# Attention and FFN in one kernel: when the products with the values are made, which PSUM banks the products share, and which engine standardises the layernorms

## Chip, core and metric

One core of a Trainium2 chip runs the whole program. The time is the device time of one execution in microseconds (us). It is told as the median of several runs; a profiled execution, of which the trace is, has a time of its own.

The engines by the names that the profile uses: PE is TensorE (matmuls; its weight loads are PEld), DVE is VectorE, ACT is ScalarE, POOL is GpSimd. SP issues all DMA transfers, in its program order.

## Reference

Sixteen sequences of 256 tokens with 256 channels go through one transformer layer, in float32:

```python
x = x + attn(layernorm(x))            # 16 heads of 128, 4 key/value heads
x = x + ffn(layernorm(x))             # one linear 256 -> 256, 8-bit integers
# attn: q, k, v = x wq^T, x wk^T, x wv^T;  scores = q k^T / sqrt(128)
#       a query sees the last 32 keys (itself among them) and the first 4 ("sinks")
#       softmax over these, times v, all heads times wo^T
# ffn:  weight rows and x rows scaled to -128..127 and rounded; integer product; scaled back; + bias
# layernorm: (x - mean) / sqrt(var + 1e-5), no weights
```

## The kernel before

**Units and visits.** A unit is one sequence n and one key/value head g with its four query heads: 64 units, numbered i = 4n + g. The main loop makes one visit for each unit but the last two (i = 0 to 61). The last two units of sequence 15 are cut by halves of the tokens instead of by heads, and stand with the rest of the end behind the loop. The kernel's order is the written order: `in_written_order` ties every engine's instructions to the order in which the program makes them. So each engine works through its own list, and waits where an operand or a buffer isn't ready.

**A visit** i, in TensorE's order:

1. `unit_scores(i)`: the scores `pss` of unit i. Queries are taken in blocks of 16 tokens, four heads at a time (64 columns of weights), against 52 keys (48 of the window, 4 sinks): 32 matmuls of 128x64 weights (L592). DVE scales and masks them into SBUF (L598) and takes the maxima (L607); ACT makes eight exponentials with their sums (L612).
2. `queries(i + 1, 0)`: two heads of the next unit's queries, `pq`. For sequences 1 to 15 a product of 2x2 blocks is made of seven block products instead of eight (`products`, `combine`, Winograd's form): seven products in two PSUM banks, 28 matmuls, since `mm` cuts each into two of 64 columns (L90). ACT copies the first product (L336), DVE makes five additions out of the banks into `qt` (L321 to L325). One such pass of five is "a half of the queries".
3. the first part of the output projection `py` of unit i - 3 (`projected_fast`, parts 0 and 1, again by seven products; 24 and 32 matmuls).
4. `times_values(i - 2)`: the products with the values, `po`: 64 matmuls with 52 rows and 64 columns of weights (L684), into two banks. ACT copies the two banks to `oT` (L695), and POOL makes four sums `os` of it (L286 to L289), which the output's second part multiplies.
5. the other half of the queries, `queries(i + 1, 1)`, then the output's second part.
6. a "chunk": in turn the keys or the values of two heads of the next sequence (`pk`, `pv`; 28 matmuls). ACT copies both banks in the next visit (`both_banks`, L342), POOL adds them up (L321 to L325), and for keys ACT spreads them into the windows `kt` (L447, L448). Values go through DRAM (`vd`) to `vw`, the layout that `po` needs.
7. every fourth visit, the FFN's product `pa`.

**Softmax's way.** `normalised` (L620 to L626) scales the exponentials by their sums on DVE and transposes them in blocks of 32 (`z`). SP stores `z` to DRAM (`zd`) and loads it back in another order (`ad`, four transfers) in the next visit (`ways`). `po` reads `ad` and `vw`.

**Layernorms.** `statistics` makes means and variances on DVE and 1/sqrt on POOL (L213 to L218); `standardise` makes (x - mean) times 1/sqrt on DVE in one operation per tile of 128 tokens (L223). That is done once for the attention (`norm`) and once for the FFN (`ffn_steps`). Both results are transposed by way of DRAM (`turned_by_blocks`: z_xnT and z_hb out, xnT and hb back). In between, the FFN's `quantise` takes DVE and POOL (L803, L806, L807), `narrow` casts `hb` on ACT (L828), `rest` scales `pa` on DVE (L848).

**Where such steps stand.** `at(place, point, f)` puts a step into visit `place` at a named point; `do` runs it there. For the FFN a `plan` lists step, visit after the sequence's output, and point.

**PSUM.** Eight banks: one for scores (`ps_s`), one for transposes and `pa` (`ps_t`), two for the output (`ps_y`), two for the queries (`ps_q`, tags q0 and q1) and two in rotation for `po`, keys and values (`ps_m`). A pool gives a buffer anew only when its last reader is done.

Of the kernel before, what the change touches and what calls it, by code (L numbers as in the profile page):

```python
# [34 lines left out]
def kernel(  # L35
# [14 lines left out]
    P = 128  # L50
# [33 lines left out]
    ps_q = ctx.enter_context(tc.tile_pool(name="ps_q", bufs=1, space=bass.MemoryType.PSUM))  # L84
    ps_m = ctx.enter_context(tc.tile_pool(name="ps_m", bufs=2, space=bass.MemoryType.PSUM))
# [122 lines left out]
    def statistics(src, tiles, tag, eng=pool):  # L208

        st = p2.tile([P, NT, nc.vector.BN_STATS_DIM], FP, tag="st", name=f"st_{tag}")  # L210
        mv = p3.tile([P, NT, nc.vector.BN_AGGR_DIM], FP, tag="mv", name=f"mv_{tag}")
        for j in tiles:
            dve.bn_stats(st[:, j, :], src[:, j, :])  # L213
        for j in tiles:
            dve.bn_aggr(mv[:, j, :], st[:, j, :])
        js = slice(tiles[0], tiles[-1] + 1)
        eng.tensor_scalar(mv[:, js, 1], mv[:, js, 1], LN_EPS, None, ALU.add)
        pool.tensor_tensor(mv[:, js, 1], mv[:, js, 1], half[:, js], ALU.pow)  # L218
        return mv
# [4 lines left out]


# [49 lines left out]

    def q_banks(name):
        return [ps_q.tile([P, 4, P], FP, tag=f"q{k}", name=f"{name}_{k}") for k in range(2)]
# [94 lines left out]
    def norm_stats(n):  # L372
        mvs[n] = statistics(xts[n], range(NT), f"a{n}")

    def norm(n, t):
        if t == 0:
            xns[n] = p1.tile([P, NT, DM], FP, tag="xn", name=f"xn_{n}")
        standardise(xns[n], xts[n], mvs[n], [t])
# [158 lines left out]
    def queries(n, g, half_of, plain=False):  # L537
# [6 lines left out]
        if n > 0 and not plain:  # L544
            p = q_banks(f"pq_{n}_{h}")
# [5 lines left out]
        if plain:  # L551
            pq = ps_m.tile([P, 4, P], FP, tag="m", name=f"pq_{n}_{h}")
        else:
            pq = ps_q.tile([P, 4, P], FP, tag=f"q{half_of}", name=f"pq_{n}_{h}")
# [23 lines left out]
    def unit_scores(i):  # L578
# [4 lines left out]
        if i == U - 1:  # L583
            pss = ps_q.tile([P, 4, P], FP, tag="q0", name=name).rearrange("p a b -> p (a b)")[:, 0 : NK2 * NK]
# [56 lines left out]
    def turned_twice(i, sm):  # L641
# [21 lines left out]
        def turn(a):  # L663
            pz = turned[a] = ps_q.tile([P, 4, P], FP, tag=f"q{a}", name=f"pz_{i}_{a}")
# [64 lines left out]
    def projected(n, g, t):  # L729
# [12 lines left out]
        if g == G - 1 and not last:  # L742
            return lambda: dve.tensor_add(xts[n][:, t, :], xts[n][:, t, :], py)

    def projected_fast(i, part):
# [16 lines left out]
        if (g, part) == (G - 1, 1):  # L762
# [3 lines left out]
            def rest():  # L766
                sums.first()
                sums.combine(dve)
# [3 lines left out]
            return rest  # L772
# [5 lines left out]
    def ffn_steps(n):  # L778
# [9 lines left out]
        def stats():  # L788
            got.append(statistics(xt, tiles, f"f{tag}"))

        def norm():
            standardise(h, xt, got[0], tiles)
# [67 lines left out]
    def last_steps(j):  # L860
# [36 lines left out]
        def turn():  # L897
            for c in range(NC):
                pt = ps_q.tile([P, 4, P], FP, tag=f"q{c}", name=f"ht_{tag}_{c}")[:, 0]
# [39 lines left out]
    VALUES, OUTPUT = 2, 3  # L939

# [9 lines left out]
    at(0, "early", lambda: norm(1, 0))  # L950
    at(0, "early", lambda: norm(1, 1))
    at(1, "turn", lambda: turned(1))
    for n in range(2, B):
        p = (n - 1) * G
        if n > 2:
            at(p - 4, "load", lambda n=n: load_x(n))
        at(p - 3 + (n == 2), "gap", lambda n=n: norm_stats(n))
        at(p - 2, "gap", lambda n=n: norm(n, 0))
        at(p - 2, "early", lambda n=n: norm(n, 1))
# [15 lines left out]
    for n in range(B - 1):  # L975
        p = n * G + G - 1 + OUTPUT
# [7 lines left out]
        if by_dma(n):  # L984
            plan = (("stats", 1, "gap"), ("norm", 1, "late"), ("scale", 2, "early"), ("quantise", 2, "early"),
                    ("turn", 3, "turn"), ("out", 3, "early"), ("back", 3, "leave"), ("narrow", 4, "late"),
# [4 lines left out]
        if n == B - 3:  # L991
            ffn_last_but_one = step
            plan = plan[:7]
# [29 lines left out]

    for i in range(U - NT):
        do(i, "load")
        if i - 1 in ways:
# [16 lines left out]
        first = queries(*units[i + 1], 0)  # L1043
# [5 lines left out]
        exps(range(1))  # L1049
        first.first() if isinstance(first, Products) else first()  # L1050
        exps(range(1, NK2))
        if isinstance(first, Products):
            first.combine(dve)
        rests, o = [], i - OUTPUT
        if o >= 0:
            if fast_output(units[o][0]):
                projected_fast(o, 0)
            else:
                rests.append(projected(*units[o], 0))
        do(i, "early")  # L1060
        values_out = times_values(i - VALUES) if i >= VALUES else None
        ways[i] = normalised(i, sm)
        if values_out:
            for f in values_out:
                f()
        second = queries(*units[i + 1], 1)
        second.first() if isinstance(second, Products) else second()
        if o >= 0:
            if fast_output(units[o][0]):
                rests.append(projected_fast(o, 1))  # L1070
            else:
                rests.append(projected(*units[o], 1))
        if isinstance(second, Products):
            second.combine(dve)
        for f in rests:
            if f:
                f()
# [10 lines left out]
        do(i, "leave")  # L1088
    assert not tasks and not waiting, sorted(tasks)
# [9 lines left out]
    exps_a(range(NK2))  # L1099
    for k in range(2):  # L1100
        normal_a(k)
    projected_fast(a - 3, 0)
    values_out = times_values(a - 2)
    values_out[0]()
    rest = projected_fast(a - 3, 1)
    rest()
    exps_b(range(NK2 // 2))
    values_out = times_values(a - 1)
    values_out[0]()
# [76 lines left out]
```

## Time and profile before

| what | value |
|---|---|
| median of 3 runs (lowest to highest) | 670.62 us (670.53 to 671.6) |
| the profiled execution's own time | 672.28 us |
| its span in the trace | 670.1 us |
| mean granted TensorE clock | 0.996 |
| DMA, mean over the span | 146 GB/s |
| mean of one po matmul (L684), of one pq matmul (128x128) | 221 ns, 273 ns |
| four visits, 300.1 to 339.4 us: DVE, ACT, POOL busy | 33.61, 23.55, 32.33 us |

How to read it: the page gives the busy time of each engine as a share of the span. TensorE's matmuls are pipelined, so 658.5 us "busy" doesn't say that each took its least time; the distance between the starts of neighbours does. The chain is followed back from the last instruction, at each step to what released it or to the instruction before it on its engine. In the timeline, neighbouring instructions of one kind are put together: start, length, engine, line, operation, tiles, how many, and in brackets an idle time of the engine before it with its releaser. "issue" as releaser means that the engine waited for nothing that the profile shows. Rows of groups give the busy time, the mean of one in ns, and the idle time before them.

### The profile page before, as it was taken

The numbers are of one execution on the slowest core, as the hardware profiler recorded it, in microseconds if no ns is written. First come the engines' busy times: TensorE is split into PE (matmuls) and PEld (weight loads), VectorE is DVE, ScalarE is ACT, GpSimd is POOL, SyncE is SP. The second block draws the span as 40 slices with busy tenths as digits, with TensorE's granted clock in tenths as the row PEclk, the third lists the DMA queues.
The fourth block names the chain that finished last, engine by engine and source line by source line (L and its number), as shares of the span: only waits on it lengthen the run. The fifth ranks groups of instructions, "written<-read, shape, count | busy, mean of one in ns | idle before, by whom it ended". The sixth has DMA issues, their size and how long they took to land.

```text
span 670.1 us, 35751 instructions
## 1 busy us (share of the span) xinstructions
PE 658.5 (98%) x14956; PEld 618.0 (92%) x14956; DVE 542.7 (81%) x1418; ACT 390.8 (58%) x1514; POOL 523.7 (78%) x795
## 2 busy tenths in 40 slices
PE   8999999999999999999999999999999999999995
PEld 6688899999999999999999999999999999999863
DVE  3766787888888898888889888888888889878665
ACT  3776465567566566655656656556756656656441
POOL 4788788787887978789787887978788797878534
PEclk9999999999999999999999999999999999999998
DMA  8558565656666566765666666566766656565520
GB/s 288 131 145 178 144 165 116 157 142 160 148 150 159 138 154 139 163 155 140 152 151 131 157 149 165 134 146 137 172 151 150 150 142 156 128 145 129 131 49 32
DMA packets 152928, 97.62 MB, mean 146 GB/s; under 512 B 69440, under 2 KB 143040, under 8 KB 152768
## 3 DMA queue, kind: packets, MB, share of 16 engines
q1 hardware_dynamic: 152768, 95.34, 59.8%
q8 instruction: 118, 1.93, 1.3%
q14 instruction: 42, 0.34, 0.2%
HBM read 59.11 MB, written 36.18 MB: 142 GB/s over the span
## 4 chain that ended last, share of the span: by engine, by line
PE 97%; issue 1%; DVE 1%; ACT 1%; POOL 0%; DMA 0%; POOLq 0%
PE pq L90 31%; PE py L90 30%; PE po L684 10%; PE pss L592 9%; PE pv L90 7%; PE pk L90 7%; PE pa L90 1%; PE pz L666 0%; ACT scores L612 0%; DMA x<-in_x_dram 0%; POOL mv_a L218 0%; ACT qt L563 0%; PE ht_last L900 0%; DVE xn L223 0%; PE pm L187 0%
## 5 line engine op out<-in xcount | busy, mean ns | idle before, releaser
L612 ACT ACTIVATE scores<-scores,nmax 128x52 f32<-128x52 f32 x512 | 166.7, 329 | 110.8 <-DVE nmax L607 108.7
L90 PE MATMUL pq<-xs,wq_sums 128*64 128x128 f32 x1416 | 118.0, 273 | 0.0
L612 ACT ACTIVATION_READ_ACCUMULATOR scores<-scores,nmax 128x1 f32 x512 | 97.1, 190 | 0.0
L90 PE MATMUL pq<-xnT,wq_sb 128*64 128x128 f32 (+1 forms) x1104 | 94.4, 295 | 0.0
L90 PE MATMUL py<-wo_sb,oT 128*64 128x128 f32 (+1 forms) x1152 | 88.9, 297 | 0.0
L90 PEld LDWEIGHTS pq<-xs,wq_sums 128*64 128x64 f32 x1416 | 86.3, 137 | 0.0
L90 PE MATMUL py<-wo_sums,os 128*64 128x128 f32 x1344 | 83.1, 273 | 0.0
L342 ACT COPY b_k<-pk 128x512 f32<-128x512 f32 (+1 forms) x60 | 31.9, 533 | 85.6 <-PE pk L90 83.6
L684 PEld LDWEIGHTS po<-ad,vw 52*64 52x64 f32 x4096 | 65.5, 134 | 12.5 <-issue 11.9
L90 PEld LDWEIGHTS py<-wo_sb,oT 128*64 128x64 f32 x1152 | 69.3, 137 | 7.5 <-issue 0.3
L90 PEld LDWEIGHTS py<-wo_sums,os 128*64 128x64 f32 x1344 | 75.4, 137 | 0.1
L684 PE MATMUL po<-ad,vw 52*64 52x64 f32 x4096 | 74.3, 221 | 0.0
L592 PE MATMUL pss<-kt,qt 128*64 128x52 f32 x2048 | 72.1, 223 | 0.6 <-issue 0.4
L592 PEld LDWEIGHTS pss<-kt,qt 128*64 128x64 f32 x2048 | 68.6, 138 | 3.6 <-ACT qt L563 1.6
L90 PEld LDWEIGHTS pq<-xnT,wq_sb 128*64 128x64 f32 x1104 | 61.6, 137 | 9.6 <-issue 0.7
L598 DVE SCALAR_TENSOR_TENSOR scores<-pss,masks 128x416 f32<-128x416 f32 x62 | 36.2, 583 | 40.7 <-PE pss L592 40.7
L695 ACT COPY oT<-po 128x512 f32<-128x512 f32 x124 | 65.4, 577 | 0.8 <-PE po L684 0.8
L323 DVE TENSOR_TENSOR qt<-pq,qt 128x256 f32<-128x256 f32 x118 | 50.2, 425 | 12.7 <-DVE qt L322 0.5
L321 DVE TENSOR_TENSOR qt<-pq,p_q 128x256 f32<-128x256 f32 x118 | 46.9, 397 | 14.4 <-ACT p_q L336 14.1
L286 POOL TENSOR_TENSOR os<-oT 128x256 f32<-128x256 f32 x56 | 42.8, 764 | 11.2 <-ACT oT L695 11.2
L623 DVE TENSOR_TENSOR scores<-scores,sm 128x416 f32<-128x416 f32 x62 | 49.3, 795 | 2.1
L447 ACT COPY kt<-k_line 128x1536 f32<-128x1536 f32 x32 | 47.3, 1477 | 0.4 <-POOL k_line L325 0.3
(186 smaller groups left out, 1564.1 us busy)
## 6 DMA issues: line engine op xcount, KB each, us to landing
vw<-vd SPq DMA_DIRECT2D x60, 336.0 KB
zd<-z SPq DMA_DIRECT2D x62, 256.0 KB
ad<-zd SPq DMA_DIRECT2D x248, 64.0 KB
vd<-vt SPq DMA_DIRECT2D x30, 256.0 KB
x<-in_x_dram SPq DMA_DIRECT2D x15, 256.0 KB
out_dram<-y SPq DMA_DIRECT2D x15, 256.0 KB
zd_xnT<-z_xnT SPq DMA_DIRECT2D x56, 64.0 KB
xnT<-zd_xnT SPq DMA_DIRECT2D x56, 64.0 KB
```

The costliest lines, as they stand in the source:

```text
L90: pe.matmul(to[c : c + HALF], left[:, c : c + HALF], right, start=start, stop=stop)
L286: pool.tensor_add(s[0], a21, a22)
L321: eng.tensor_add(c11_u, like(p[0][:, 0:2], c11_u), two(p1, c11_u))
L323: eng.tensor_add(c21_c22, like(p[1][:, 0:2], c21_c22), v.unsqueeze(1).to_broadcast(c21_c22.shape))
L342: act.copy(copies[k], self.p[k][:, 0 : 4 - k])
L447: act.copy(k[:, :, :, 0:NW], windows())
L592: pe.matmul(pss[j * HALF : (j + 1) * HALF, k, :], qt[n, g][:, t, bt].rearrange("p h i -> p (h i)"), kt[n, g // 2][:, g % 2, b, :], start=T ...
L598: dve.scalar_tensor_tensor(s[:, :, 0:NK], pss, SCALE, masks, ALU.mult, ALU.add)
L612: act.activation(s[:, k, 0:NK], s[:, k, 0:NK], AF.Exp, bias=nmax[:, k : k + 1], scale=1.0, accum_out=sm[:, k : k + 1],)
L623: dve.tensor_mul(s[:, :, 0:NK], s[:, :, 0:NK], sm.unsqueeze(2).to_broadcast([P, NK2, NK]))
L684: pe.matmul(po[j][d0 : d0 + HALF, k].rearrange("p (a y) -> p a y", a=2), vw[n, g // 2][r, kb, v0 : v0 + HALF], ad[k][r], start=True, stop= ...
L695: act.copy(to[:, j], po[j].rearrange("p k (h i) -> p k h i", i=QB))
```

## The change

- **Products with values.** Odd visits from 3 on make `po` of two units (i - 3 and i - 2) right after each other; even visits make none. Behind the loop, units 60 and 61 are made together as well. The output is one unit later: an even visit makes both parts of unit i - 4 and part 0 of unit i - 3, an odd one part 1 of unit i - 4.
- **Queries.** Both halves of the next unit's queries come at the start of the visit, ahead of the output; DVE adds them up one after the other.
- **PSUM.** `ps_q` is gone; `ps_m` has four banks in rotation for queries, `po`, keys, values and the transposes of the end.
- **Layernorm.** From the third sequence on, and in every FFN that goes through DRAM, ScalarE standardises: per tile one operation that adds the negated mean and one that multiplies. POOL negates the mean.
- **Places.** Statistics and norm move by a visit or to another point, and x is loaded a visit earlier; the FFN's steps are put elsewhere, and some of those of sequences 12 and 13 go behind the loop. The `ad` of a unit whose number is even is loaded at the end of the odd visit that follows it.

```diff
-    ps_q = ctx.enter_context(tc.tile_pool(name="ps_q", bufs=1, space=bass.MemoryType.PSUM))
-    ps_m = ctx.enter_context(tc.tile_pool(name="ps_m", bufs=2, space=bass.MemoryType.PSUM))
+    ps_m = ctx.enter_context(tc.tile_pool(name="ps_m", bufs=4, space=bass.MemoryType.PSUM))
...
+        if negated:
+            pool.tensor_scalar(mv[:, js, 0], mv[:, js, 0], -1.0, None, ALU.mult)
...
+    def standardise_act(dst, src, mv, tiles):
+
+        for j in tiles:
+            act.activation(dst[:, j, :], src[:, j, :], AF.Identity, bias=mv[:, j, 0:1], scale=1.0)
+        for j in tiles:
+            act.mul(dst[:, j, :], dst[:, j, :], mv[:, j, 1:2])
...
-            p = q_banks(f"pq_{n}_{h}")
+            p = m_banks(f"pq_{n}_{h}")
...
-        at(p - 3 + (n == 2), "gap", lambda n=n: norm_stats(n))
-        at(p - 2, "gap", lambda n=n: norm(n, 0))
-        at(p - 2, "early", lambda n=n: norm(n, 1))
+        at(max(p - 4, 1), "early", lambda n=n: norm_stats(n))
+        at(p - 2, "early", lambda n=n: norm(n))
...
-        p = n * G + G - 1 + OUTPUT
+        p = n * G + G + 3
...
-            plan = (("stats", 1, "gap"), ("norm", 1, "late"), ("scale", 2, "early"), ("quantise", 2, "early"),
-                    ("turn", 3, "turn"), ("out", 3, "early"), ("back", 3, "leave"), ("narrow", 4, "late"),
+            plan = (("stats", 1, "early"), ("norm", 2, "early"), ("scale", 2, "late"), ("quantise", 2, "late"),
+                    ("turn", 3, "early"), ("out", 3, "early"), ("back", 3, "leave"), ("narrow", 4, "late"),
                     ("linear", 5, "linear"), ("rest", 7, "early"), ("leave", 7, "leave"))
...
+    def output_parts(i):
+
+        if i % 2:
+            return [(i - 4, 1)]
+        return [(i - 4, 0), (i - 4, 1), (i - 3, 0)]
...
     for i in range(U - NT):
+        visit = i % 2 == 1 and i >= 3
         do(i, "load")
-        if i - 1 in ways:
+        if i - 1 in ways and not visit:
             ways.pop(i - 1)()
...
+        ps.append(queries(*units[i + 1], 1))
+        done = 0
+        for k, q in enumerate(ps):
+            exps(range(done, 1 + 3 * k))
+            done = 1 + 3 * k
+            q.first() if isinstance(q, Products) else q()
+        exps(range(done, NK2))
+        for q in ps:
+            if isinstance(q, Products):
+                q.combine(dve)
         do(i, "early")
-        values_out = times_values(i - VALUES) if i >= VALUES else None
+        rests = [r for r in (output_part(*o) for o in output_parts(i) if o[0] >= 0) if r]
+        for r in rests:
+            r[0]()
+        values_out = [times_values(u) for u in (i - 3, i - 2)] if visit else []
+        for r in rests:
+            r[1]()
         ways[i] = normalised(i, sm)
-        if values_out:
-            for f in values_out:
+        for k, v in enumerate(values_out):
+            for f in v:
                 f()
-        second = queries(*units[i + 1], 1)
...
         do(i, "leave")
+        if i - 1 in ways:
+            ways.pop(i - 1)()
...
     exps_a(range(NK2))
+    ffn_last_but_one("turn")
+    ffn_last_but_one("out")
+    ffn_last_but_one("back")
+    ffn_last_but_two("rest")
+    ffn_last_but_two("leave")
     for k in range(2):
         normal_a(k)
-    projected_fast(a - 3, 0)
-    values_out = times_values(a - 2)
-    values_out[0]()
-    rest = projected_fast(a - 3, 1)
-    rest()
+    for part in range(2):
+        output_part(a - 4, part)
+    output_part(a - 3, 0)
+    values_out = [times_values(u) for u in (a - 2, a - 1)]
+    for v in values_out:
+        v[0]()
+    for f in output_part(a - 3, 1):
+        f()
     exps_b(range(NK2 // 2))
-    values_out = times_values(a - 1)
-    values_out[0]()
```

## Prediction

> **What bounds the kernel now.** I read the page first: the share of each engine, and the chain that ended last.
>
> ```profile
> PE 658.5 (98%) x14956; PEld 618.0 (92%) x14956; DVE 542.7 (81%) x1418; ACT 390.8 (58%) x1514; POOL 523.7 (78%) x795
> ...
> PE 97%; issue 1%; DVE 1%; ACT 1%; POOL 0%; DMA 0%; POOLq 0%
> ```
>
> TensorE is the whole chain. So an edit pays only if it shortens TensorE's stream, and costs only if it makes TensorE wait. The wait table of the weight loads shows one wait that repeats:
>
> ```profile
> PEld po L684 <- issue: 11.9, 62, 0.4
> ```
>
> Sixty-two times, once a visit, the products with values (po) begin 0.19 us late for no releaser that the trace shows. The PE timeline of one visit says what surrounds them:
>
> ```profile
> 303.55 0.61 PE L90 MATMUL py<-wo_sums,oT 128*64 128x128 f32 x8
> 304.08 1.16 PE L684 MATMUL po<-ad,vw 52*64 52x64 f32 x64
> 305.17 0.66 PE L90 MATMUL pq<-xnT,wq_sb 128*64 128x128 f32 x8
> 305.66 0.61 PE L90 MATMUL pq<-xs,wq_sums 128*64 128x128 f32 x8
> 306.10 0.39 PE L90 MATMUL pq<-xs,wq_sb 128*64 128x128 f32 x4
> ```
>
> Eight matmuls of the 128x64 shape take 0.44 us where nothing changes (305.66 to 306.10), but 0.53 ahead of po and 0.49 behind it: the 52x64 shape costs at both ends. The start stamps of single matmuls give it exactly. Pairs of 128x64 matmuls follow each other at 102 ns (last start to first), groups of four po at 38. Into po it is 203 (101 too many), between po's first two groups 87 (49 too many), out of po 148 (110 over 38), between the first two pairs behind it 153 (51 too many). Together **0.31 us for each stretch of po**. A po stretch is alone its shape: 64 of them.
>
> A second thing: every fourth visit the score matmuls (pss) wait inside their stretch, 975 ns long instead of 869, because DVE's last sums of the queries end too late:
>
> ```profile
> 339.93 1.26 PE L592 MATMUL pss<-kt,qt 128*64 128x52 f32 x32
> ...
> 340.16 0.29 DVE L325 TENSOR_TENSOR qt<-pq,qt 128x128 f32<-128x128 f32 x1
> ```
>
> The sums of `qt` still run at 340.45 while the scores that read `qt` started at 339.93. That is 0.106 us in most of 14 places.
>
> **The change, part by part.**
>
> *Two units' po together.* The loop's 60 units come in 30 pairs (odd visits 3 to 61), and units 60 and 61 make one more behind the loop: 31 stretches fewer. 31 x 0.31 = **-9.6 us**. All of it lies on TensorE's path. If the second unit's 64 kept their own slow first group (49 ns) and were joined at 102 instead of 38 (64 ns more), 0.197 would be left, -6.1; I take 0.31, because within a stretch all later groups stand 38 apart.
>
> *Both halves of the queries early.* DVE sums both halves right after each other, some 3 us before the next scores. The 14 waits of 0.106 go: **-1.5** (bounds 0 and -1.8, with one longer wait at 70 us).
>
> *What the new order asks of the banks.* Per odd visit PE now writes ten banks from a rotation of four: q first (A,B), q second (C,D), po (A,B), po (C,D), chunk (A,B). I lay a clock from the visit's first pss matmul, with strides from the timeline: pss 0.92, 28 matmuls 1.54 or 1.53, 32 py 1.75 plus 0.10 entry, po 0.94 + 0.04. First po at 5.84, second at 6.82, chunk at 7.87, end 9.44. An even visit (80 py) takes 9.88, with pa 10.32. Four visits: 39.08, against 39.82 now (for instance 300.11 to 339.93): the same 0.74.
>
> DVE's side of the clock, from the rows of the visit that starts at 310.03:
>
> ```profile
> 310.03 1.09 PE L592 MATMUL pss<-kt,qt 128*64 128x52 f32 x32
> ...
> 311.17 0.59 DVE L598 SCALAR_TENSOR_TENSOR scores<-pss,masks 128x416 f32<-128x416 f32 x1 [0.94 <-PE pss L592]
> ...
> 312.47 0.34 ACT L612 ACTIVATE scores<-scores,nmax 128x52 f32<-128x52 f32 x1 [1.75 <-DVE nmax L607]
> ...
> 313.09 0.42 DVE L321 TENSOR_TENSOR qt<-pq,p_q 128x256 f32<-128x256 f32 x1 [0.18 <-ACT p_q L336]
> ```
>
> The first sums begin at 3.06; five of them take 1.77 and the next follow at 1.72, so the second half is done at 6.6. The first po (5.84) finds A,B free at 4.85; the second (6.82) finds C,D free 0.2 us ahead. That holds where DVE and ACT enter the visit on time. In the visit with g = 3 they don't: DVE carries y, two transposes and the normalisation of the visit before to its end, ACT two key and two value copies (1.57 + 0.96), so both start some 0.3 late, and the sums end at 6.9. I charge 0.2 in 14 visits, **+2.8** (bounds 0 and 0.4 each: 0 to 5.6).
>
> *Layernorm on ScalarE.* Two sequences' worth (attention and FFN) leave DVE per four visits: 2 x 2 x 0.62 to 0.80 (L223), off the path. ACT takes eight operations of 128x256 with a per-partition operand instead. No row shows one. Nearest rows:
>
> ```profile
> L612 ACT ACTIVATE scores<-scores,nmax 128x52 f32<-128x52 f32 x512 | 166.7, 329 | 110.8 <-DVE nmax L607 108.7 <-DVE st_f L213 2.0
> ...
> L704 ACT COPY oT<-po 128x256 f32<-128x256 f32 x8 | 2.4, 386 | 2.2 <-PE po L684 2.2
> ```
>
> L612 has such an operand; with 204 more columns at 0.84 ns (577 ns at 512 against 255 at 128) one is 0.50 long. Four L704 copies follow at 0.30. Four operations lie between 1.2 and 2.3 us; since L612 hides the read behind it (stride 0.325) I take 0.43 each, 1.7. The FFN's four stand in an odd visit (g = 1), between the exponentials (end at 5.36) and the copies of po, which can begin at 5.84 + 1.16 = 7.0: ACT is free at 7.1. The chunk wants bank A at 7.87, and gets it at 7.65. So nothing; the first block's second half of TensorE work (po of the second unit) hides it by 0.2, and each 0.1 us beyond costs 14 x 0.1 = 1.4. POOL gains one negation of two columns (0.22, L217's size) per layernorm, 0.44 in 39 us.
>
> [...]
>
> *Transfers.* SP's queue keeps its order within a visit; the two `ad` loads of a pair now wait at the end of an odd visit and the start of the next for buffers that the pair of po frees (8 us into the odd visit), and are read two visits later. Behind them stand vw (read three visits later) and zd_hb. The tightest is hb: zd_hb issued from 8.6 of visit g = 2, landed 4.5 us later, read back in 2.6 behind the `out` store, landed at some 8 of visit g = 3, where ACT casts it at 9.2. So nothing, by 1 us; if it is gone, ACT holds up the chunk's copies behind it, and the next queries.
>
> *The ends.* In the first visits the output and po of sequence 0 come one visit later, so visits 1 to 3 are shorter on TensorE while POOL makes weight sums (3.2 us each); what is lost there is in the bounds below. Output products of one more unit (56 matmuls, 3.05 us) move behind the loop, so the loop is shorter by as much; there they fill the 1.3 us in which PE waits for its transposes at 638.7. Against it, the FFN of sequence 13 now turns behind the loop: zd_hb, hb and the cast come through SP's queue behind four ad and six vw transfers. POOL's h is done some 5 us into the tail, SP reaches zd_hb at 6, writes 2.8, 2.7 to land (606.9 to 609.6 for zd), reads back 2.6 plus 2: 15.5 to 16.5 with the cast, where PE wants it at 15.3. **+0.7** (-1.5 to +3).
>
> Sum: -9.6 - 1.5 + 2.8 + 0.7 = **-7.6**. The profiled execution took 672.28 (span 670.1 and 2.2 around it), so 664.7; the median of three is 670.62, so **663.0**.
>
> **Rivals.**
>
> *Slower: POOL's queue reaches ScalarE's, and TensorE waits once in four visits.* Now POOL makes one unit's sums os a visit; afterwards two in a row, 5.8 us, and the key chunk's sums stand behind them. Place: sequence's second half. From the start of visit g = 1: ACT's layernorm 5.36 + 1.7 = 7.1; two po copies 8.1; eight os 13.9 (2.9 a unit, L286 to L289); h clipped and shifted 16.4 (2.4, L806, L807); key sums 19.4 (3.04, L321 to L325); key copies on ACT 21.0 (1.57, L447, L448); value-chunk copy 21.6; and its bank is what the second half of the queries wants in visit g = 3 at 9.44 + 9.88 + 2.46 = 21.8. The margin is 0.15. For it: POOL is 78% busy, and the layernorm row is missing from the trace. Against: each link is a measured stride but one. If the four operations take 2.4 and each POOL group its worst row (3.11 twice, 3.12), it is 1.2 late, 1.05 past the margin, 14 x 1.05 = +14.7: 677.7. It decides from 0.54 late past the margin (7.6/14).
>
> *Smaller gain: the switch isn't removed but moved.* The second po stretch waits for its banks at 0.4, and its first group is slow again (0.197 x 31 = 6.1): -6.1 - 1.5 + 5.6 + 0.7 = -1.3, 669.3. For it: four banks for ten uses. Against: DVE loses 2.4 to 3.2 us of layernorm per four visits.
>
> *Nothing (the change doesn't do what it says):* the 0.31 is a cost of po's own 64, not of the turn of shapes; then -1.5 + 0.7 and 0 to 2.8 are left, 669.8 to 672.6. Against: the start stamps show 203 into the 128x128 transposes (pa to pz) and 202 out of them too.
>
> **Numbers.** Forecast 659 to 667: 0.64. Small gain, 667 to 669.3: 0.16. Within 0.2% (what a measurement of this kernel can tell): 0.06. Slower: 0.14. Range 659 to 671: it leaves most of the slower case out, and reaches the forecast's lower bound (-9.6 - 1.8 - 0.2).
>
> **What would show it.** The wait of po for "issue" some 33 times instead of 62; po stretches of 128 with one 203 ahead; four visits in 39.1 to 39.4 us; no wait in pss. Wrong, if PE waits at pq for ACT b_v (g = 3), at po for DVE qt, or at pa in the tail for hT.

## The result, and the profile after

| what | before | after |
|---|---|---|
| median, same chip (lowest to highest) | 671.42 us (670.53 to 672.6) | 728.98 us (724.5 to 733.91) |
| ratio, 95% interval | | 1.0858 [1.0806, 1.091] |
| profiled execution, its span | 672.28, 670.1 us | 732.36, 730.6 us |
| mean granted TensorE clock | 0.996 | 0.966 |

The forecast was 663.0. The change costs 58 us instead of saving 8. The page of after, engine shares and then the chain:

```profile
PE 682.7 (93%) x14956; PEld 643.3 (88%) x14956; DVE 527.6 (72%) x1362; ACT 438.5 (60%) x1626; POOL 532.6 (73%) x823
...
PE 55%; DVE 16%; DMA 13%; SPq 6%; ACT 6%; issue 3%; POOL 1%; DVEq 0%; ACTq 0%; POOLq 0%
```

TensorE does the same 14956 matmuls, but it is only 55% of the chain, where it was 97%. A chain that leaves the busiest engine for DVE, DMA and SP's queue says that something else now sets the end. The wait table of after (total us, times, longest) names it:

```profile
DVE z_xnT L405 <- DMA zd_hb<-z_hb: 42.4, 12, 5.0
...
PEld po L685 <- ACT p_q L341: 18.2, 12, 2.5
...
PEld po L685 <- issue: 16.5, 29, 1.3
```

Po has 29 unexplained waits instead of 62 (the forecast said some 33), but longer ones; and VectorE waits twelve times, 3.5 us each, to transpose xn until the store of z_hb has landed. The two have nothing to do with each other in the computation. DVE's timeline of one visit of after shows the place:

```profile
387.62 0.70 DVE L405 STREAM_TRANSPOSE z_hb<-h 128x512 f32<-128x512 f32 x1
...
393.05 0.71 DVE L405 STREAM_TRANSPOSE z_xnT<-xn 128x512 f32<-128x512 f32 x1 [2.67 <-DMA zd_hb<-z_hb]
393.69 0.55 DVE L599 SCALAR_TENSOR_TENSOR scores<-pss,masks 128x416 f32<-128x416 f32 x1
```

SP's timeline of the same stretch of after:

```profile
388.35 2.18 SPq L410 DMA_DIRECT2D zd_hb<-z_hb  x4
```

`turned_by_blocks` takes z from `p1` under the tag "zx" for both transposes, and `p1` has one buffer for a tag. So z_xnT may be written only when zd_hb has carried z_hb away: issued from 388.35, landed at 393.0. In before the two transposes stood in different visits, 17 us apart, and no transpose waited for the buffer:

```profile
303.46 0.71 DVE L401 STREAM_TRANSPOSE z_hb<-h 128x512 f32<-128x512 f32 x1
...
320.44 0.70 DVE L401 STREAM_TRANSPOSE z_xnT<-xn 128x512 f32<-128x512 f32 x1
```

The change runs the FFN one visit later, so z_hb ("early") and z_xnT ("late") meet in visit g = 2 of every sequence. Behind the waiting transpose DVE's queue holds the next visit's masking, maxima and query sums, and these hold the banks that po needs. TensorE's timeline of another such visit of after:

```profile
261.74 0.33 PE L685 MATMUL po<-ad,vw 52*64 52x64 f32 x4 [1.63 <-ACT p_q L341]
262.79 1.22 PE L685 MATMUL po<-ad,vw 52*64 52x64 f32 x64 [0.72 <-DVE qt L330]
264.50 1.97 PE L685 MATMUL po<-ad,vw 52*64 52x64 f32 x60 [0.49 <-DVE qt L330]
266.40 1.12 PE L89 MATMUL pk<-xnT,wk_sb 128*64 128x128 f32 x8
```

TensorE idles 2.84 us, and then the 60 po and the chunk take twice their time: the chain gives 3.18 us for the 28 matmuls of pk, against 1.53 in before. The windows (length; busy and count of PE, PEld, DVE, ACT, POOL; clock; DMA share; GB/s) say why:

```profile
264.40:269.60 5.20, 5.10 (x92) 5.01 (x94) 3.78 (x9) 2.75 (x6) 4.48 (x6) 0.50 0.24 73
```

The granted clock is 0.50 there, and up to 271.1. So in this visit the wait is paid twice. The clock falls so in eight of the twelve visits that wait: they take 15.0 us on the mean, the other four 12.8, and the same visits take 10.1 where the wait is gone (`zx2`, below). Visit lengths of after, from one visit's first pss to the next, four to a row (g = 0 to 3), two rows:

```
after   10.32   9.67   9.88  15.56
        11.10   9.67   9.88  12.39
```

The first three are close to the forecast's clock (10.32, 9.44, 9.88, 9.44 for the four; the 11.10 holds the end of the low clock); twelve visits of g = 3 take 12.3 to 15.9.

### The profile page after: what moved, and what is told of

The parts are those of the page before. It is cut to its first block, busy times and chain, and to the rows that moved or that the text cites. A ratio compares the mean times of both kernels' runs of the same rounds, so it can differ in the third digit from the quotient of the medians.

```text
span 730.6 us, 35713 instructions
## 1 busy us (share of the span) xinstructions
PE 682.7 (93%) x14956; PEld 643.3 (88%) x14956; DVE 527.6 (72%) x1362; ACT 438.5 (60%) x1626; POOL 532.6 (73%) x823
## 4 chain that ended last, share of the span: by engine, by line
PE 55%; DVE 16%; DMA 13%; SPq 6%; ACT 6%; issue 3%; POOL 1%; DVEq 0%; ACTq 0%; POOLq 0%
PE pq L89 15%; PE py L89 15%; PE pk L89 7%; PE po L685 7%; DMA vw<-vd 7%; DMA zd_hb<-z_hb 6%; PE pss L593 6%; SPq L638 4%; PE pv L89 4%; ACT scores L613 3%; DVE qt L328 2%; DVE qt L326 2%; DVE qt L327 1%; DVE nmax L608 1%; DVE qt L330 1%
## 5 line engine op out<-in xcount | busy, mean ns | idle before, releaser
L685 PE MATMUL po<-ad,vw 52*64 52x64 f32 x4096 | 87.5, 233 | 34.0 <-DVE qt L330 14.7
L685 PEld LDWEIGHTS po<-ad,vw 52*64 52x64 f32 x4096 | 78.9, 144 | 45.0 <-ACT p_q L341 18.2
L291 POOL TENSOR_TENSOR os<-oT 128x256 f32<-128x256 f32 x56 | 45.8, 818 | 78.4 <-ACT oT L696 78.4
L89 PE MATMUL pq<-xnT,wq_sb 128*64 128x128 f32 (+1 forms) x1104 | 92.2, 291 | 2.5 <-ACT b_v L347 1.5
L326 DVE TENSOR_TENSOR qt<-pq,p_q 128x256 f32<-128x256 f32 x118 | 49.6, 420 | 40.1 <-ACT p_q L341 40.1
L89 PEld LDWEIGHTS pq<-xnT,wq_sb 128*64 128x64 f32 x1104 | 64.8, 137 | 10.7 <-ACT b_v L347 5.1
L593 PEld LDWEIGHTS pss<-kt,qt 128*64 128x64 f32 x2048 | 71.9, 142 | 1.5 <-ACT qt L564 1.0
L294 POOL TENSOR_TENSOR os<-oT,os 128x256 f32<-128x256 f32 x56 | 47.3, 845 | 0.0
L89 PE MATMUL pq<-xs,wq_sb 128*64 128x128 f32 x472 | 46.8, 273 | 0.0
```

The lines of the kernel that those rows point to most:

```text
L89: pe.matmul(to[c : c + HALF], left[:, c : c + HALF], right, start=start, stop=stop)
L291: pool.tensor_add(s[0], a21, a22)
L294: pool.tensor_sub(s[3], a12, s[1])
L326: eng.tensor_add(c11_u, like(p[0][:, 0:2], c11_u), two(p1, c11_u))
L593: pe.matmul(pss[j * HALF : (j + 1) * HALF, k, :], qt[n, g][:, t, bt].rearrange("p h i -> p (h i)"), kt[n, g // 2][:, g % 2, b, :], start=T ...
L685: pe.matmul(po[j][d0 : d0 + HALF, k].rearrange("p (a y) -> p a y", a=2), vw[n, g // 2][r, kb, v0 : v0 + HALF], ad[k][r], start=True, stop= ...
```

## Experiments

**Theories.** A: the one z buffer makes nearly all of the loss. B (rival): POOL's sums of two units in a row make it, by way of the key copies. C (rival): the layernorm on ScalarE makes it, by ScalarE's longer queue. For what A leaves: P, the pair of units costs something itself; D, TensorE's instructions arrive too slowly within a long stretch of short products; E, the POOL chain of the forecast's first rival, and the ends.

### Two buffers of z, and one buffer with the transposes apart

`zx2` (tiles of the end change places with others to make room):

```diff
-        z = p1.tile([P, NQ, NT * NC, BL], FP, tag="zx", name=f"z_{tag}")
+        z = p2.tile([P, NQ, NT * NC, BL], FP, tag="zx", name=f"z_{tag}")
```

> The changed kernel with two buffers instead of one for z, the tile that the block transposes of both layernorms write (room is made by putting three small tiles of the start and the end into other buffers). Theory A (z_xnT on VectorE waits for the store of z_hb out of the one buffer, and everything behind it on VectorE is late, once in four visits): the visits with g = 3 shrink from 12.3 to 15.9 us to about 9.7, twelve of them, some 55 us in all: 669 to 677 us. Theory B (POOL's two units of sums in a row delay the key copies and through them the value chunk's banks): the buffer does nothing, over 715.

Measured: 683.81, ratio 1.0165 [1.0146, 1.0184]. 45 us come back, the wait for zd_hb is gone from the table, and the clock is 0.993. B is out for these 45, and A holds for them; but the time is above A's 669 to 677, so more is left than was expected.

`xnT_later`, one buffer, z_xnT one visit later:

```diff
-        at(p - 2, "late", lambda n=n, way=way: way.extend(turned_by_blocks(...)))
-        at(p - 1, "load", lambda way=way: way[0]())
+        at(p - 1, "early", lambda n=n, way=way: way.extend(turned_by_blocks(...)))
+        at(p - 1, "early", lambda way=way: way[0]())
```

> The changed kernel with one z buffer, but the transpose z_xnT (and its store) one visit later, early in the visit with g = 3 instead of at the end of the one with g = 2, by when z_hb has been stored. Theory A: the wait is gone or under 1 us, 668 to 682 us. Theories B and C: no change, over 715.

Measured: 685.68, 1.0194 [1.0163, 1.0225]: nearly the same by another way, again above the range expected (668 to 682). It is the meeting in one visit, not the buffer's place in memory.

### Is it the layernorm?

`ln_dve`: the changed kernel with `standardise` on DVE in both places, one z buffer.

```diff
-        (standardise_act if n > 1 else standardise)(xns[n], xts[n], mvs[n], range(NT))
+        standardise(xns[n], xts[n], mvs[n], range(NT))
```

> The changed kernel with the layernorms standardised by VectorE again (one operation a tile, no negation), everything else as changed, one z buffer. Theory A: the wait for the store stays, and VectorE gets 2.5 to 3 us more work in four visits: 722 to 740 us. Theory C (ScalarE's eight operations more, ahead of the copies of po, are what TensorE waits for): under 690.

Measured: 748.48, 1.1141 [1.1106, 1.1176], another 20 us slower, and above A's 722 to 740. C is out as the main cause. The profile shows where most of the rest comes from: VectorE's own standardising stands ahead of the transpose z_hb, which begins 9.4 us into its visit on the mean instead of 7.8 in after, so z_xnT, behind the store, comes later too. The twelve visits that wait are 8.5 us longer in sum, of the 13.2 by which the profiled spans differ (743.8 and 730.6). `before_ln_act` is the reverse, the old order with ACT's layernorm:

> The order of before, with the layernorms standardised by ScalarE alone; each half of norm is still a step of its own, so nothing else moves. Forecast's step (the four ScalarE operations cost TensorE nothing): 669.5 to 672.5 beside before on the same chip, and POOL waits for them no longer than in before. Rival (the longer layernorm, about 1.2 to 2.3 us against VectorE's, holds POOL and through it the key sums, also in the old order): slower by 0.5 to 1 us in each of some 13 sequences, so 677 to 684.

Measured: 676.02, 1.0069 [1.0057, 1.0081]: 4.9 us, neither theory's size. Where? From the third sequence on, four visits take 39.82 as in before, with a stray 0.3 to 0.7 here and there. One visit of the start is longer, 13.11 against 8.66; the granted clock is 0.50 there from 37.5 to 40.9, which it isn't in before. The chain of before_ln_act there:

```profile
34.53 0.72 POOL mv_a L220
35.25 0.02 issue
35.27 0.51 ACT xn L232
35.78 0.85 ACT b_k L351 x2
...
40.38 0.51 ACT xn L232
40.89 0.48 ACT oT L704
41.37 0.04 issue
41.42 1.75 PE pv L90 x28
```

ScalarE stops for the statistics that POOL is late with, and the copies that TensorE waits for stand behind. So in the old order the layernorm costs next to nothing in the steady state, and once at the start. The changed order takes those statistics earlier: with it (`zx2`) the ninth pss begins 0.7 us sooner than in before.

### What does a stretch of po cost?

`before_cut`: before, po cut in two by the output's first part in 56 units.

```diff
         for k, (g, kb) in enumerate(blocks(i)):
+            if between and k == NK2 // 2:
+                between()
```

> The kernel before, with each unit's 64 products with the values cut in two by the first output part (24 matmuls of the other shape), in the 56 units with the fast output: 56 stretches more, no work more. If a stretch costs the 0.31 us of the forecast by the turn of shapes: +17 us, 688. If part of the 0.31 belongs to the waits ahead of the first product and not to the shape: 0.2 to 0.26 each, +11 to +15. If the cost isn't one of shapes: within 2 us of 671.4.

Measured: 684.86, 1.018 [1.0162, 1.0199], +12.1. TensorE's timeline of before_cut:

```profile
308.65 0.69 PE L686 MATMUL po<-ad,vw 52*64 52x64 f32 x32
309.27 1.09 PE L90 MATMUL py<-wo_sb,oT 128*64 128x128 f32 x16
310.20 0.61 PE L90 MATMUL py<-wo_sums,oT 128*64 128x128 f32 x8
310.74 0.69 PE L686 MATMUL po<-ad,vw 52*64 52x64 f32 x32
```

Visits that were 9.82 and 10.25 are 10.13 and 10.56: 0.31 for each further stretch, the forecast's number. (56 x 0.31 is 17.4. The visits of 9.92 grow by 0.21 only, since their pss wait goes, 1.4 in all, and the tail is 1.3 shorter, which leaves 14.7; the spans differ by 13.5, so 1.2 isn't accounted for.) By the total, 12.1, a stretch would cost 0.22, which the expectation gave to the waits; but the second halves have no wait ahead of them and are entered at 202 ns like the first ones. In the visits, the turn of shapes has the price that I gave it.

`before_twice`: each unit's 64 po made twice in one stretch, the same values.

```diff
-        for k, (g, kb) in enumerate(blocks(i)):
+        for k, (g, kb) in [*enumerate(blocks(i))] * (2 if i < U - NT else 1):
```

> The kernel before, with each of the 62 units' 64 products with the values made twice in one stretch (the second pass writes the same values over the first; nothing is left out). No new waits, no new shapes: 64 more po cost 0.94 + 0.05 us, 62 of them +61, 733 us. Theory D: on top, gaps of 0.4 to 1.5 us inside po stretches that end 1.3 to 1.5 us after a 16 KB instruction packet has landed, 10 to 30 us in all: 743 to 765 us. Without theory D: 728 to 737.

Measured: 747.17, 1.1138 [1.1113, 1.1163], +76. The 64 more take 0.934 us each time (a stretch of 128 is 1.877 from first to last start), 58 in all. Some 18 are left, most of it in gaps without a releaser, but not where theory D had them: inside the stretches they come to 2 us, and most stand behind, ahead of the queries (0.7 us in before) and of the output:

```profile
PEld pq L90 <- issue: 10.3, 16, 3.1
PEld py L90 <- issue: 3.3, 6, 1.4
```

The trace has 149 instruction packets of 16 KB where before has 118 (more on packets below). The 13 idle times of TensorE in the loop that have no releaser and are over 0.15 us end 1.3 to 1.8 us after such a packet landed. Joining 64 to 64 is thus smooth where the second 64 has nothing to wait for, and the longer stretches bring gaps with the packets, mostly behind them.

### The pair itself

`zx2_single`: one unit's po in every visit, with the output one unit earlier again and the tail's order to match; the rest of the change as it is.

```diff
-        if i % 2:
-            return [(i - 4, 1)]
-        return [(i - 4, 0), (i - 4, 1), (i - 3, 0)]
+        return [(i - 3, 0), (i - 3, 1)]
...
-        values_out = [times_values(u) for u in (i - 3, i - 2)] if visit else []
+        values_out = [times_values(i - 2)] if visit else []
```

> The changed kernel with two buffers of z, but one unit's products with values in every visit (unit i-2, behind both output parts of unit i-3), so that no po stretch is longer than 64 products; the four banks, the early second queries, the layernorm on ScalarE and the later steps of the FFN stay. It tells apart what the pair costs from what the rest costs. Theory P (the pair itself costs: 0.19 us of semaphore instructions between its units, 31 times, -5.8; 6 to 8 us of gaps from the supply of instructions; against 31 stretches more at 0.217, +6.7): 675 to 681, no 187 ns in the stretch, gaps in po below 2 us in sum. Theory E (it is the POOL chain ahead of the second queries and the two ends that cost, whatever the pair does): 683 to 692, since the stretches come back and nothing goes.

Measured: 676.51, 1.0082 [1.0063, 1.01]. P holds: the pair, forecast to save 9.6, makes the kernel slower by 5.6 (the ratios of 1.0165 and 1.0082), together with the later output that belongs to it. An undisturbed pair in zx2:

```profile
430.02 2.33 PE L685 MATMUL po<-ad,vw 52*64 52x64 f32 x128
432.28 0.66 PE L89 MATMUL pk<-xnT,wk_sb 128*64 128x128 f32 x8
```

First to last start is 2.111 us, where 128 of them took 1.877 in before_twice. The missing 0.23 stands ahead of the second unit's first products: four instructions of 51 ns that do nothing but wait for semaphores (the second unit's four `ad` loads, ScalarE, VectorE). `zx2_early` takes them out, by letting TensorE wait for both units' loads earlier, among longer matmuls:

```diff
+        if visit and isinstance(ps[1], Products):
+            for u in (i - 3, i - 2):
+                pe.matmul(ps[1].p[1][0:HALF, 3, 0:1], ident[:, 0:HALF], ads[u][0][:, 0, 0:1], start=True, stop=True)
```

> The changed kernel with two buffers of z; behind the second queries of each visit with a pair, two products of 64 x 1 read one column of each unit's ad (into a place of the queries' bank that nobody reads), so that TensorE has waited for the four loads of each ad before the short products begin. Ahead of the second unit's first po only VectorE's and ScalarE's semaphores are left. Theory S (the 187 ns ahead of the second unit are the instructions that wait for semaphores): an undisturbed pair from first to last start 1.92 to 1.98 us instead of 2.11, -4 to -5.8 us in 31 pairs, against 62 small products of 0.03 to 0.08 each, +2 to +5: 679 to 685 in all. Rival (a new pair of banks costs the 187 ns, whoever waits): 2.11 us as before, and 685 to 689.

Measured: 683.06, 1.0177 [1.0164, 1.019]. The pair is 1.894 long, 0.217 shorter: the waits were the cost. But the undisturbed visits stay 9.68 and 9.88, since the small products take as much. The waits can be moved, not saved, in this way.

`zx2_apart` and `zx2_parts22` change what stands around the pair: both output parts of unit i - 4 in every visit, in zx2_apart with the second part between the two units' po.

```diff
-        if i % 2:
-            return [(i - 4, 1)]
-        return [(i - 4, 0), (i - 4, 1), (i - 3, 0)]
+        return [(i - 4, 0), (i - 4, 1)]
```

> As zx2, but the two units' products with the values no longer in one stretch: every visit makes both output parts of unit i - 4, and in odd visits the second part (32 matmuls of 128x64) stands between the first and the second unit's 64. Theory D (TensorE's instructions come in packets of 16 KB, 256 instructions; 128 po with their 128 loads use up a whole packet in 2.1 us, faster than the next arrives, so it stands still in the middle of a stretch, 0.4 to 1.4 us, seven times in zx2; and the second unit's four waits, 51 ns each, can't be read ahead of time): gaps inside po and the 0.187 in front of the second unit vanish (-7 to -8 and -5.6), 30 turns of shape come back (+6.5, at the 0.217 of the cut): 673 to 680 us. If the stretch is worth its 0.31 and the gaps have another cause: 690 or more.

> As zx2_apart, but both output parts ahead of the two units' po, which stay one stretch of 128. Tells the order of the output from the cut. VectorE's sums of the second half of the queries are done long before the second unit's po. If the 0.187 us ahead of its third group is the wait for these sums, it vanishes (-5.6 us, 678); if it is the four semaphore instructions on TensorE's own queue, it stays, as do the gaps inside po: 680 to 688.

zx2_apart: 681.95, 1.0165 [1.0142, 1.0189], above the 673 to 680 of theory D. The stretches are 0.943 again and the second unit's waits hidden, but 7 us of gaps in po remain, and the stretch of 0.31 is back: no gain. The gaps aren't all of one kind. Of the six over 0.5 us, three end 1.4 to 1.6 us after an instruction packet landed, as in theory D. In the other three, TensorE's semaphore instruction stands until VectorE's last sum of the queries (`qt`, L330) is done: the first po comes earlier in these visits, and the forecast's wait for the banks is there. In 27 odd visits such an instruction ends with that sum, 10.8 us in all over the 51 ns that each takes otherwise. zx2_parts22: 694.24, 1.0347 [1.033, 1.0364], also outside what was expected, and its waits (us, times, longest) show a cause of its own:

```profile
PEld pq L89 <- ACT b_v L347: 20.2, 14, 1.7
```

This is the forecast's slower rival, in all 14 places: even visits are 1.3 us shorter there, so the second queries ask for their bank 1.3 us sooner, and the chain through POOL ends when it did.

### The POOL chain

In zx2 the same wait is 4.5 us:

```profile
PEld pq L89 <- ACT b_v L347: 4.5, 9, 1.7
```

The chain of zx2 ahead of a second half of the queries:

```profile
359.13 1.50 POOL h L806
360.63 0.71 POOL k_line L326
...
363.18 0.72 POOL k_line L330
363.90 0.02 issue
363.92 1.48 ACT kt L451
365.40 0.20 ACT kt L452
365.59 0.49 ACT b_v L347
366.09 0.04 issue
366.13 1.75 PE pq L89 x28
```

Link by link it is the forecast's chain, and its margin is gone by 0.3. `zx2_clip` puts the FFN's clipping behind the key sums on POOL:

```diff
-                    ("turn", 3, "early"), ("out", 3, "early"), ("back", 3, "leave"), ("narrow", 4, "late"),
+                    ("clip", 3, "pool"), ("turn", 3, "late"), ("out", 3, "late"), ("back", 4, "load"), ("narrow", 5, "early"),
```

> As zx2, but POOL clips and shifts the FFN's values behind the sums of the key chunk instead of ahead of them (2.4 us), and what follows (z_hb, hb, the cast) comes as much later. The forecast's slower rival (os, os, clip, key sums, key copies, value copies, bank of the second queries) then loses 2.4 us of its chain: TensorE's waits at pq for b_v, 0.26 to 0.45 us in every visit with g = 3, vanish: -3 to -6, 678 to 681 us. If they have another cause: no change (682 to 686).

Measured: 681.77, 1.0164 [1.0139, 1.0188] beside 1.0165 of zx2: a miss. In its profile the waits are gone but one, visits of g = 3 take 9.7 instead of 10.0 and the span is 678.6; the median doesn't show the 4 us beyond doubt. Before took 672.73 beside zx2 and 671.02 beside zx2_clip, so the difference is -2.0 by the times and nothing by the ratios; and the four runs of zx2_clip are 680.3, 680.4, 683.2 and 683.6, of which the profile shows a short one. Of the 4.5 us between the profiled spans, 3.5 lie in visits of g = 3 and 1.2 in the tail.

### Gaps that nobody releases

TensorE's timeline of one pair in zx2:

```profile
226.98 2.10 PE L685 MATMUL po<-ad,vw 52*64 52x64 f32 x113
230.31 0.46 PE L685 MATMUL po<-ad,vw 52*64 52x64 f32 x15 [1.23 <-issue]
```

Behind the first pair, seven of 30 are longer than 2.111 by over 0.25 us, 6.9 us in sum: six by gaps without a releaser, and the shortest (0.27) by a wait for a transfer. The trace's DMA records have a queue of kind "instruction" with 118 packets of 16 KB; over 14956 matmuls and as many loads that is 64.6 bytes each, and the 7936 more of before_twice took 31 packets more, 64.0 bytes each: by this estimate 256 to a packet. In these six a packet landed 1.3 to 1.5 us before the gap ended (here at 228.97). A pair and its loads are 256 instructions, one whole packet by the estimate, used up in 2.1 us; on the mean a packet lasts 5.8 (683.1 us for 118). Two runs moved all instructions by half a packet and by a whole one (64 instead of 32 products):

```diff
+    for _ in range(32):
+        pe.matmul(warm[0:HALF, 0:1], ones[:, 0:HALF], ones[:, 0:1], start=True, stop=True)
```

> The changed kernel with two buffers of z, and 32 products of 64 x 1 ahead of all work (each is recorded as two matmuls and two loads, so 128 instructions of TensorE, half a packet of 16 KB at 64 bytes each). In the unshifted kernel 7 pairs behind the first, the pairs 1, 5, 9, 13, 17, 21 and 26, hold gaps of 0.27 to 1.46 us. Theory D (a gap comes where a packet of instructions runs out within a pair): at most 2 of those 7 pairs have a gap over 0.25 us here, and others have them. Rival (the gaps come from the work of that visit, from transfers or other engines): the same 7 pairs, or nearly so, and the same sum.

> As the shift by half a packet, with 64 products of 64 x 1: 256 instructions, a whole packet. Theory D: the gaps lie at the same pairs as without a shift, at least 5 of the 7 pairs 1, 5, 9, 13, 17, 21 and 26, and few others. Rival (the gaps move whenever anything is added at the start): other pairs, as with half a packet.

Pairs longer than an undisturbed one by over 0.25 us, behind the first pair:

```
zx2               1   5      9     13     17     21        26
zx2_shift_half        7     11     15     19     23  24
zx2_shift_whole       5      9     13            21        26
```

The whole packet leaves the gaps at their pairs (five of the six without a releaser, and no new one); the half moves every one. A half-shifted pair:

```profile
192.81 1.65 PE L685 MATMUL po<-ad,vw 52*64 52x64 f32 x88
195.43 0.45 PE L685 MATMUL po<-ad,vw 52*64 52x64 f32 x12 [0.96 <-issue]
```

So D holds for the gaps in pairs: they follow the boundaries of packets, not the work. (The times, 691.91 and 696.21, have the small products at the start in them, 0.2 us each, and say nothing.) What sets when the next packet comes, no run shows.

### What is left without the pair

`single_clip_tail` joins zx2_single, zx2_clip and one step of the tail, `ffn_last_but_one("linear")`, set behind `projected(n, 1, 0)`. `single_ffn` has the FFN's steps and the tail of before:

```diff
-        p = n * G + G + 3
+        p = n * G + G + 2
```

> One unit's products in every visit, the FFN's clipping on POOL behind the key sums, and the last but one FFN's matmul one output part later in the tail. If what is left of the loss after the pair is undone lies in the POOL chain (0.3 us in each of 13 visits) and in the wait of 2.5 us for hT in the tail, this is 4 to 7 us below the kernel with single units, 669 to 676, at the time of before. If the POOL chain costs nothing net (as moving the clip did not lower the time measurably), 0 to 3 us below it.

> One unit's products in every visit, as in the run with single units, and the FFN's steps one visit earlier, so that the tail is that of before. What is left of the change: four banks in rotation, both halves of the queries early, layernorms on ScalarE. By the single run, whose visits are 0.1 us per four shorter than those of before and whose tail is 2.3 us longer: 672 to 675. A version that beats before would need under 669; the 0.1 us per four visits, 1.5 us in all, is the most there is to be had: 670 at best, which is the same as before.

Measured: 674.48, 1.0052 [1.0036, 1.0067], and 673.15, 1.0035 [1.0021, 1.0049]. By the ratios single_clip_tail is 2 us below zx2_single, as expected for a POOL chain that costs nothing net. single_ffn's four visits are 39.71 against 39.82, and its last pss begins 1.6 us before that of before; its tail, which begins there, is 41.6 long against 39.1. In its chain that tail waits for `vw`, whose loads stand on SP behind four loads of hb and four of ad. `single_tail` puts hb behind them and gives po and output parts the tail order of before; `before_back` moves hb alone, in before:

```diff
     for f in stores:
         f()
+    ffn_last_but_one("back")
```

> One unit's products in every visit, the FFN one visit earlier, and a mended tail: the four loads of hb of the last but one FFN behind those of ad and vw on SP, and the first products of the tail between the two output parts, as in before. If the 2.5 us that the tail is longer than that of before are the late loads of ad and vw: 2 to 3 us below the run with single units and the earlier FFN, which was 673.2 beside 671.0 of before, so 670 to 671, ratio 0.996 to 1.000. If the tail waits for something else: 672 to 674.

> Before, with the same move of the four loads of hb behind those of ad and vw in the tail. TensorE waits 1.14 us in the tail of before, for a pz that no engine releases, and VectorE 1.27 us for vw; if the loads of ad and vw 3 us earlier are worth anything there, 669.5 to 671; if pa then waits for hb, 671 to 674.

Measured: 672.33, 1.0012 [1.0, 1.0024], and 671.65, 1.0013 [1.0001, 1.0024]. By the ratios single_tail is 1.5 us below single_ffn, less than the 2 to 3 expected, and its profiled tail is no shorter: 41.65, with a clock of 0.50 from 645.0 to 648.4, and its chain now goes by vw and hb to pa. That the late vw makes the longer tail is so not shown. In before_back the move gains nothing. No version beats before: four banks, early queries and ScalarE's layernorm together are worth nothing that can be measured.

## Why the prediction was wrong

- **The step that failed** is "Transfers ... So nothing, by 1 us". It followed zd_hb only as far as its reader hb and asked which buffers the loads wait for, but not which buffer the *source* of the store blocks. z_hb and z_xnT share one; the diff moved the one into the other's visit. The step's times were right (issued 8.8 us into visit g = 2, landed 4.7 later in the visit shown above); what they mean for the buffer was left out, and none of the three rivals has it. Measured: 42.4 us of waits, and a clock of 0.50 behind eight of the twelve; 45 us come back with a second buffer.
- **The 0.31 per stretch** was right (before_cut). **The sum -9.6 for the pair** was not. An undisturbed pair gives some 0.2 of its 0.31 back to instructions that wait for semaphores (zx2_early; the odd visit is 9.67, not 9.44), and the supply of instructions takes some 7 us (6.9 us in seven of zx2's pairs, six of them by gaps; the shifts). Even visits take the 9.88 and 10.32 of the forecast's clock. My lower bound, 0.197, reckoned with a slow first group and a join, not with waits in the second unit's first products. Against single units the pair comes to +5.6, with the work that it moves into the tail.
- **The pss waits, -1.5:** gone as forecast, and in the sums of single_ffn, which has no pair: 0.11 per four visits, 1.5 in all.
- **Banks, +2.8:** hardly there in the order that was forecast; zx2 has 1.2 us of po waiting for qt, in its first pair. In zx2_apart the wait is real.
- **Layernorm on ScalarE:** an operation takes 0.45 (forecast 0.43), as this group of after says:

```profile
L230 ACT ACTIVATE xn<-x,mv_a 128x256 f32<-128x256 f32 x28 | 12.6, 500 | 0.0
```

  That it hides by 0.2 held for the chunk's bank, not for the chain behind it: that is **the slower rival**, whose margin of 0.15 became a wait of 0.3 in g = 3 (4.5 us in all), below its price of 14.7 and its point of decision. It was a true mechanism with a small part in the loss.
- **The ends, +0.7:** +5.2 in zx2. The tail is 5.9 longer, and the ninth pss only 0.7 sooner, though 3.05 us of work left the start. It was not bound by TensorE there, so the work that moved away was next to no gain, and where it went it cost in full. Some 1.7 of the tail's 5.9 are a clock of 0.50 from 656.2 to 659.6, behind the wait for hT. The wait at pa for hT (2.5 us) is the one that the prediction named.
- **The sum for zx2**, by spans (683.1 against 670.1): start -0.7, tail +5.9, undisturbed visits -3.8, chain through POOL +4.3, gaps in po of those visits +6.7: +12.4 of 13.0.
- **What would show it:** 29 issue waits (forecast 33) and no wait in pss came true, and "PE waits at pq for ACT b_v" and "at pa for hT" both appeared. The signs named were all waits of TensorE; the one that mattered first was VectorE's own. (The range's lower end reckons -0.2 for the ends, though their own bound was -1.5; the miss is on the other side.)

Left open: what makes the longer tail of the versions with single units, and why the clock fell behind some of the waits and not behind others.

## What to carry to other kernels

Where a step is moved, list for each tile that it writes who else draws on that tag in the same visit, and how long the last reader, a store too, holds it (zd_hb held z_hb 4.7 us from its issue in after). A gain per stretch read from start stamps is true only if the joined stretch asks for nothing new: count the semaphores of the second half's first instructions (without four of them the pair was 0.217 us shorter in zx2_early, of a forecast 0.31). Work that leaves a stretch which isn't bound by the busiest engine need not be a gain there, and is paid for where it arrives (3.05 us left the start of zx2, which got 0.7 shorter, and the tail got 5.9 longer).

## What the runs showed of the hardware

- Products of 52x64, 15 ns each with their loads (before_twice: 128 starts in 1.877 us), ran through a 16 KB packet of instructions, 256 by the estimate above, in 2.1 us (zx2's undisturbed pair, 2.111). In 17 pairs of zx2 and the two shifts TensorE stood for 0.6 to 1.5 us and went on 1.2 to 1.6 us after the next packet had landed.
- An instruction that only waits for a semaphore took 51 ns on TensorE's queue (337 of them in zx2), and among the short products of a pair four of them cost 0.19 to 0.23 us (zx2 against zx2_early and before_twice). Behind a change of shape (zx2_apart: entry 202 ns with the waits, as before_cut's second halves without any) they were hidden.
- In after the granted clock fell to 0.50 behind eight of the twelve waits, four times for 3.41 and four times for 6.83 us by the clock records of its trace. TensorE was idle for 2.1 to 3.0 us in these visits, in pieces of at most 2.3 us; in the four visits that kept a clock of 1.00 it was idle for 1.9 to 3.0. So the idle time of the visit alone didn't decide. These eight falls began 44.37 or 88.75 us apart.
